# Pre-norm transformer layer, one core: more of the fourth batch's query projections in the first attention slot, LayerNorm passes earlier, output projections in three interleaved portions

## The chip, the cores and the metric

The kernel runs on one core of a Trainium2 chip. A core has a matrix engine (TensorE, PE in the profile, its weight loads PEld), a vector engine (VectorE, DVE), an activation engine (ScalarE, ACT), a general engine (GpSimd, POOL), a sequencer that issues most of the transfers here (SyncE, SP), and 16 DMA engines. Each engine runs its own instructions in the order in which they were written, and waits at an instruction until the semaphores that it names have the values it wants. SBUF is the on-chip memory; matmuls write to PSUM, a small memory of banks.

The metric is the time of one launch on the device in microseconds (us), the median of several runs; lower is better. The profile comes from one more execution, which has a time of its own.

## The reference

One transformer layer on x of 4 batches × 512 tokens × 512 channels, all in fp32:

```python
def reference(x, Wq, Wk, Wv, Wo, W_gate, W_up, W_down):
    x = x + attention(layernorm(x), Wq, Wk, Wv, Wo)
    x = x + ffn(layernorm(x), W_gate, W_up, W_down)
    return x

# attention: 32 query heads and 8 key/value heads of 16 channels, T = 512
q, k, v = (h @ Wq), (h @ Wk), (h @ Wv)          # 512x512, 512x128, 512x128
q, k = q * cos + rotate_half(q) * sin, k * cos + rotate_half(k) * sin
att = where(causal, q @ k.T / sqrt(16), -inf)   # four query heads share a key head
out = (softmax(att) @ v) @ Wo
# ffn: F = 1376
y = (silu(h @ W_gate.T) * (h @ W_up.T)) @ W_down.T
```

The layernorm has no scale or shift; eps is 1e-5.

## The kernel before

**The slots.** After an opening, attention runs in four *slots*, one for each batch (`slot(b, steps)`). A slot has eight *groups* of four heads, numbered 0 to 31 over all batches. A group has four *visits* and a `last_visit`, then `averages`. In a visit PE computes two kinds of scores into PSUM (`both_scores`): `plain` (L993), queries by keys, of the group two ahead, from which DVE only takes a minimum of each row (`greatest`, L1039; it becomes the softmax's shift), and `less` (L1006), keys by queries, of the current group, from which ACT takes the exponentials (`exponentials`, L1094) and POOL clears what is above the diagonal (`causal`, L1099). `averages` (L1121) multiplies the exponentials with the values; DVE later transposes the result and takes reciprocals (`read`, L1135 and L1138), and after each second group it turns the finished heads into `cx[m]` (four tiles `cx[0]` to `cx[3]`, one for two groups). `masked` (L978, POOL) prepares the queries of a group three ahead.

**The gaps.** After the scores of visit n stands `gap(n)`, in which PE does other work: a slot gets a list of *steps*, each with a cost in microseconds that was written by hand, and a gap takes steps from its front (`fill`) until the share `shares[n]` of the list's total is used up. In slot 0 there are four gaps to a group; in slots 1 to 3 there is a fifth, `gap(4)`, after the averages. Slot 0's list (`early`) holds projections of batches 1, 2 and 3 (`rest1`, `rest2`, `rest3`), slots 1 to 3 hold the output projection and the FFN of the batch whose attention is done. Slots 1 to 3 end their attention two groups ahead in the scores, so the list is what fills the rest of PE's time.

**A projection** (`projections`, `projected`): the normalised rows, transposed (`xnT`), by a weight, 512 × 128 at a time, in eight steps of 0.43 (four narrow matmuls, eight matmul records in the profile; L299). Keys come first, then the queries of the first part, the values, and the queries of parts 1 to 3. The finished product is rotated: DVE steps `sines` (L358) and `cosines`, with multiplications and additions on POOL (L359); the keys are then spread by four POOL operations (L425). These steps stand in the queue `full` until an odd moment takes them (`odd_steps`) or until a new product needs a bank (`emptied`).

**PSUM.** `bank()` (L187) gives a product one of three buffers (`ps_mm`, 512 columns each) for everything that is not scores or averages: projections, output projections, FFN. Six more such buffers' room goes to scores and averages.

**The LayerNorm of batch 2** is made in twelve passes on ACT with the power on POOL (`quietly`: sum a, square b, scale c for each of four tiles), which stand in `calm`; `odd_steps` takes one per call. That of batch 3 is made by DVE (`statistics`, L218; `normalised`, L226) with the power on POOL (L221); batches 1 and 3 are transposed by DVE and four writes to DRAM for each tile (`flipped`, L318, issued by SP), read back as `xnT` (L320). Batch 2 is transposed by PE (`turned2`).

**The output projection** (`attended`): for each of four token tiles i, four products m (`cx[m]` by `wo_sb`, 0.85 us each) into one bank, in two portions of 1.72; then DVE adds the result to the rows (`add`, L515), and statistics, normalisation and flip of that tile (`both_steps`) go to the queue `aside`. Each product first runs all that stands in `later` (the reading of the last averages and the turning into `cx`). For batch 0 the output projection stands in slot 1 (groups 8 on), for batch 1 in slot 2 (groups 16 on), for batch 2 in slot 3 (groups 24 on), for batch 3 in the last stage, which has no attention. The last queries of batch 3 (`rest3[-24:]`, parts 1 to 3) also stand at the front of slot 1, and before the FFN the first weights are loaded by SP (`load_f(0)`, L176).

Of the kernel before, what the change touches and what calls it, by code (L numbers as in the profile page):

```python
# [22 lines left out]
NT = T // P  # L23
# [51 lines left out]
def preln_block_kernel(  # L75
# [59 lines left out]
    first, second, one16, one0 = (rope_sb[:, 2 * T + n : 2 * T + n + 1] for n in range(4))  # L135
# [44 lines left out]
    thin = [True]  # L180
# [4 lines left out]
    def emptied(n):  # L185
        for _ in range(n):
            for _, step in full.popleft():  # L187
                step()

    def bank():  # L190
        emptied(max(len(full) - (2 if copied[0] else 1), 0))
        return ps_mm.tile([P, T], F32, tag="mm", name="mm")
# [6 lines left out]
    def load_xr(b, i):  # L199
        nc.sync.dma_start(out=xr[b, i], in_=x[b, ts(i, P), :])  # L200
# [13 lines left out]
    def statistics(src):  # L214
        st = small.tile([P, 6], F32, tag="st", name="st")
        mv = small.tile([P, 2], F32, tag="mv", name="mv")
        rstd = small.tile([P, 1], F32, tag="rstd", name="rstd")
        nc.vector.bn_stats(st, src)  # L218
        nc.vector.bn_aggr(mv, st)
        nc.vector.tensor_scalar(rstd, mv[:, 1:2], EPS, None, ALU.add)  # L220
        nc.gpsimd.tensor_tensor(rstd, rstd, neghalf, ALU.pow)  # L221
        return src, mv, rstd
# [24 lines left out]
    calm = deque()  # L247
# [3 lines left out]
    aside, later = deque(), deque()  # L251
# [3 lines left out]
    def do(queue, n=1):  # L255
        for _ in range(min(n, len(queue))):
            queue.popleft()[1]()
# [61 lines left out]
        for a in [i - 1, i] if i == last else [i - 1] if i > 0 else []:  # L319
            nc.sync.dma_start(out=dst[:, :, ts(a, P)], in_=flip[n].rearrange("(k p) t -> p k t", p=P)[:, :, ts(a, P)])  # L320

    def portions(products, finish, n=2):

        made = {}

        def part(a):
            if a == 0:
                made["ps"] = bank()
            for step in products[len(products) * a // n : len(products) * (a + 1) // n]:
                step(made["ps"])  # L330
            if a == n - 1:
                left = deque(finish(made["ps"]))
                if left:
                    full.append(left)
                if not thin[0]:
                    emptied(len(full))

        return [lambda a=a: part(a) for a in range(n)]
# [153 lines left out]
    def attended(b, by_pe=()):  # L492

        found, xn, ready = {}, {}, []

        def measure(i):
            found[i] = statistics(xr[b, i])

        def norm(i):
            xn[i] = work.tile([P, D], F32, tag="xa", name="xn", bufs=4)  # L500
            normalised(xn[i], found[i])

        def flip(i):
            if i not in by_pe:
                flipped(xn[i], i, b % 2, xnTs[0], last=NT - 1 - len(by_pe))
            ready.append(i)

        def outp(i):
            def product(ps, m):
                do(later, len(later))  # L510
                product_of(ps, cx[m][:, ts(i, P)], wo_sb[:, m, :], m == 0, m == 3)

            def finish(ps):
                def add():
                    nc.vector.tensor_tensor(xr[b, i], ps, xr[b, i], ALU.add)  # L515
                    aside.extend(both_steps(measure, norm, flip, [i]))

                return [(0.69, add)]

            return [(1.72, step) for step in portions([lambda ps, m=m: product(ps, m) for m in range(4)], finish)]  # L520

        def tail():
            while NT - 1 not in ready:
                do(aside)
            for i in by_pe:
                transposed(xn[i], i, xnTs[0])

        def begin():
            if b > 0:
                for i in range(NT):  # L530
                    load_xr(b, i)

        first = [(0.0, begin), *(step for i in range(NT) for step in outp(i))]
        return first, [(0.45 * len(by_pe), tail)]

    wgu = {}

    def load_f(f):
        if f < whole:
            wgu[f] = shared[:, (f + 2) % 3, :, :, :]  # L540
            for a, w in enumerate((wg, wu)):
                load_w(wgu[f][:, a, :, :], w[:, ts(f, P)])
# [76 lines left out]
    def after(step):  # L619
        return 0.0, step  # L620
# [552 lines left out]
    begin3, turned3, rest3, _ = projections(3, 3)  # L1173
    begin2, turned2, rest2, load2 = projections(2, 2)
    begin1, turned1, rest1, _ = projections(1, 1, then=load2)
    begin, turned, start, _ = projections(0, 0, early=True)
# [29 lines left out]
    def fill(steps, upto, done):  # L1206
        while steps and done + steps[0][0] / 2 <= upto:
            cost, step = steps.popleft()
            step()
            done += cost  # L1210
            if not thin[0]:
                do(aside)
        return done
# [5 lines left out]
    for h in range(2):  # L1219
        for n, entries in enumerate((((0, 3),), ((0, 2), (3 * P, 0)), ((0, 1),))):  # L1220
            for c, i in entries:
                for r in range(4):
                    plain_score(h, r, i, pairs[r // 2][:, r % 2, c : c + P * (i + 1)])
            for r in range(4):
                for c, i in entries:
                    greatest(h, r, i, pairs[r // 2][:, r % 2, c : c + P * (i + 1)])
            if n == 2:
                turned_round(h)
            odd_steps((1.5, 1.0, 2.7 - h)[n])
            if h == 0:  # L1230
                nc.gpsimd.memset(values(n + 1), 1.0)
            done = fill(opening, each * (h + (0.3, 0.68, 1.0)[n]), done)
        if h == 0:
            laid_out(0)
            masked(2)
# [3 lines left out]
    def slot(b, steps):  # L1239

        steps = deque(steps)
        total = sum(cost for cost, _ in steps)
        done, part = 0.0, 0.0
        groups = range(8 * b, 8 * b + 8)
        thin[0] = copied[0] = b == 0
        narrow[0] = True

        shares = (0.2, 0.225, 0.2875, 0.2875, 0.0) if thin[0] else (0.19, 0.19, 0.22, 0.22, 0.18)

        def upcoming(n):  # L1250

            upto, us = part + total * shares[n] / 8, 0.0
            for cost, _ in steps:
                if done + us + cost / 2 > upto:
                    break
                us += cost
            return us

        def gap(n):
            nonlocal done, part  # L1260
            part += total * shares[n] / 8
            pool_steps((3, 2, 2, 0, 3)[n])
            done = fill(steps, part, done)

        for g in groups:
            h = g + 2
            laid_out(g + 1)
            for n, visit in enumerate(visits):
                e = (e0, e0, e1, e1)[n]
                if h < len(GROUPS):  # L1270
                    both_scores(h, g, visit)
                    exponentials(e[:, slice(0, 2) if n % 2 else slice(2, 4), :], less)
                elif n % 2 == 0:
                    both_scores(h, g, visit)
                    exponentials(e[:, 2:4, :], less)
                    exponentials(e[:, 0:2, :], plain)
                if n == 1:
                    causal(e0, 0)
                if n == 3:
                    causal(e1, 0)  # L1280
                    causal(e1, 3 * P, exchanged=True)
                all_greatest(h, visit)
                holding[0] = n == 3
                if thin[0]:
                    odd_steps((1.3, 0.95, 0.95, 1.05)[n], (2, 1, 1, 0)[n])
                else:
                    odd_steps(min(0.8 * upcoming(n) - (0.4, 0.4, 0.8, 0.8)[n], 2.3))
                gap(n)
            last_visit(h, g)
            turned_round(h)  # L1290
            averages(g)
            odd_steps(1.4)
            if not thin[0]:
                gap(4)
        thin[0] = copied[0] = narrow[0] = False
        emptied(len(full))
        if b == B - 1:
            do(later, len(later))
        for cost, step in steps:
            step()  # L1300
# [9 lines left out]
    def restored():  # L1310
        nc.scalar.dma_start(out=homes[1], in_=spill)

    turns = [step for pair in zip(turned2, *[iter(rest1[-8:])] * 2) for step in pair]
    early = [*rest1[16:-8], *turns, begin3, *rest2, *turned3, *rest3[:-24]]
    for u in range(whole):
        early.insert(4 * u + 4, after(lambda u=u: copies(u)))
    slot(0, early)
# [1 line left out]
    before, behind = attended(0, by_pe=(2, 3))  # L1319
# [18 lines left out]
    for u in range(whole):  # L1338
# [3 lines left out]
        asides += [(at + 1.0 * n, lambda n=n, combine=combine: combine(n)) for n in range(4)]  # L1342
    asides += [(6.0, spilled), (34.0, load_down), (34.1, load_rest)]
    start1 = [
        before[0],
        *rest3[-24:-12],
        *before[1:],
        after(lambda: load_f(0)),
        *rest3[-12:-1],
        *behind,  # L1350
        rest3[-1],
# [16 lines left out]
    before, behind = attended(1)  # L1368
# [15 lines left out]
    before, behind = attended(2)  # L1384
# [3 lines left out]
    before, behind = attended(3)  # L1388
# [36 lines left out]
```

## Time and profile before

| what | value |
|---|---|
| time, median of 3 runs (lowest to highest) | 847.44 us (846.82 to 847.46) |
| time of the profiled execution | 848.06 us |
| span of the profiled execution | 845.8 us |
| granted TensorE clock, mean | 1.00 |
| opening, until group 0's first scores | 0 to 49.8 us |
| slot 0 (groups 0 to 7) | 49.8 to 173.6, 123.8 us |
| slot 1 (groups 8 to 15) | 173.6 to 357.7, 184.1 us |
| slot 2 (groups 16 to 23) | 357.7 to 536.0, 178.3 us |
| slot 3 (groups 24 to 31) | 536.0 to 667.5, 131.5 us |
| last stage | 667.5 to 845.8, 178.3 us |

A line of the timeline has the start in us, the duration in us, the engine, the line of the code, the operation, its output and input by the program's names with their shapes, and how many instructions are drawn together; in brackets the engine's idle time just before it and what ended it. "SPq" is the queue of SyncE. PE instructions that follow each other at once on several parts of the array are drawn with overlapping times.

### The profile page before, as it was taken

What the parts mean: (1) busy time and instruction counts of PE and PEld (TensorE: products, weight loads), DVE (VectorE), ACT (ScalarE), POOL (GpSimd) and SP (SyncE); (2) the same over time, 40 slices, a digit from 0 to 9 for tenths busy, and PEclk for the clock granted to TensorE, in tenths of its full rate; (3) what the DMA queues carried; (4) which work ended last, traced back from release to release, by engine and by line L of the source; (5) the groups of instructions that cost most, each with busy time, mean ns of one, the idle gap of its engine ahead of it and who ended that gap; (6) DMA issues with size and microseconds to landing.
All of it is one profiled execution on the core that took longest, in us unless ns stands there. A gap on an engine that the chain in (4) does not pass through costs nothing.

```text
span 845.8 us, 28256 instructions
## 1 busy us (share of the span) xinstructions
PE 822.5 (97%) x11980; PEld 452.2 (53%) x11980; DVE 545.5 (65%) x1601; ACT 231.3 (27%) x342; POOL 352.5 (42%) x514
## 2 busy tenths in 40 slices
PE   6999999999999999999999999999999999999998
PEld 5654444544333335333555555436655556788887
DVE  7877777778555554458677776686877633656632
ACT  1045654422232322222233232222323331011100
POOL 4575574773544344223265634532244444101130
PEclk9999999999999999999999999999999999999999
DMA  8533304003764742253344632325333534545811
GB/s 259 124 96 78 91 16 91 5 3 64 232 191 144 235 137 77 88 200 77 84 155 140 196 115 66 115 47 151 96 97 103 162 106 148 119 146 174 291 33 50
DMA packets 149517, 101.57 MB, mean 120 GB/s; under 512 B 59696, under 2 KB 137264, under 8 KB 149136
## 3 DMA queue, kind: packets, MB, share of 16 engines
q1 hardware_dynamic: 149104, 94.01, 38.3%
q10 hardware_dynamic: 288, 5.77, 1.8%
q8 instruction: 94, 1.54, 0.8%
q14 instruction: 31, 0.25, 0.1%
HBM read 78.32 MB, written 25.17 MB: 122 GB/s over the span
## 4 chain that ended last, share of the span: by engine, by line
PE 76%; DVE 12%; POOL 4%; DMA 3%; issue 2%; ACT 1%; SPq 1%; POOLq 0%; DVEq 0%; ACTq 0%
PE mm L299 38%; PE mm L296 14%; PE sc L993 12%; DVE junk L1039 6%; PE av L1121 6%; PE sc L1006 4%; PE mm L590 2%; POOL e L1099 1%; DMA shared<-packed 1%; PE mm L582 1%; DVE st L218 1%; DVE rot L358 1%; ACT e L1094 1%; POOL home L425 1%; POOL qa L978 1%
## 5 line engine op out<-in xcount | busy, mean ns | idle before, releaser
L1039 DVE CUSTOM_DVE_ANT_0 junk<-sc,mask 128x128 f32<-128x128 f32 (+3 forms) x512 | 251.2, 491 | 139.0 <-PE sc L1006 78.4
L1094 ACT ACTIVATE e<-sc 128x1024 f32<-128x1024 f32 (+1 forms) x192 | 165.5, 882 | 384.4 <-PE sc L1006 300.7
L299 PE MATMUL mm<-xnT,shared 128*32 128x256 f32 (+1 forms) x3520 | 244.2, 420 | 2.3 <-DMA shared<-in_wg 1.5
L1099 POOL TENSOR_SCALAR_AFFINE_SELECT e<-e 128x512 f32<-128x512 f32 (+2 forms) x192 | 105.7, 560 | 225.4 <-ACT e L1094 222.3
L299 PEld LDWEIGHTS mm<-xnT,shared 128*32 128x32 f32 x3520 | 116.9, 110 | 113.0 <-issue 62.8
L993 PE MATMUL sc<-home,qa 32*64 32x512 f32 (+6 forms) x2048 | 156.1, 421 | 6.5 <-DVE low L1039 3.0
L1006 PE MATMUL sc<-qa,home 32*64 32x512 f32 (+6 forms) x2048 | 152.2, 427 | 1.5 <-DVE low L1039 0.8
L993 PEld LDWEIGHTS sc<-home,qa 32*64 32x64 f32 x2048 | 66.8, 131 | 90.2 <-DVE low L1039 29.1
L1121 PE MATMUL av<-e,home 128*32 128x512 f32 (+3 forms) x1024 | 81.9, 438 | 1.8 <-POOL e L1099 1.6
L296 PE MATMUL mm<-xnT,shared 128*128 128x256 f32 x360 | 80.3, 383 | 1.0 <-DMA shared<-packed 1.0
L296 PEld LDWEIGHTS mm<-xnT,shared 128*128 128x128 f32 x360 | 68.3, 192 | 12.8 <-issue 2.2
L299 PE MATMUL mm<-wd_sb,home 128*32 128x256 f32 (+3 forms) x848 | 71.4, 470 | 0.0
L1006 PEld LDWEIGHTS sc<-qa,home 32*64 32x64 f32 x2048 | 58.8, 130 | 22.5 <-issue 8.7
L1121 PEld LDWEIGHTS av<-e,home 128*32 128x32 f32 x1024 | 30.5, 109 | 47.2 <-issue 35.0
L299 PEld LDWEIGHTS mm<-wd_sb,home 128*32 128x32 f32 (+1 forms) x848 | 28.2, 110 | 36.9 <-issue 28.2
L299 PE MATMUL mm<-wo_sb,cx 128*32 128x512 f32 x384 | 45.4, 595 | 0.0
L797 POOL TENSOR_TENSOR wd_sb<-home 128x256 f32<-128x256 f32 x15 | 11.4, 759 | 75.6 <-DVE home L721 75.3
L1039 DVE DVE_READ_ACCUMULATOR2_ANT low<- 128x1 f32 x512 | 42.4, 83 | 0.0
L221 POOL TENSOR_TENSOR rstd<-rstd,neghalf 128x1 f32<-128x1 f32 x24 | 16.0, 667 | 56.8 <-DVE rstd L220 56.7
L1145 POOL TENSOR_TENSOR inv<-us,inverse 128x256 f32<-128x256 f32 x32 | 20.9, 654 | 44.5 <-DVE inverse L1138 44.3
L359 POOL TENSOR_TENSOR rot<-rot,rope_sb 128x512 f32<-128x512 f32 x18 | 25.7, 1425 | 23.0 <-DVE rot L358 22.8
L721 POOL TENSOR_TENSOR home<-home,u 128x512 f32<-128x512 f32 x20 | 25.2, 1281 | 21.2 <-DVE u L757 21.2
(146 smaller groups left out, 855.6 us busy)
## 6 DMA issues: line engine op xcount, KB each, us to landing
shared<-packed SPq DMA_DIRECT2D x90, 256.0 KB
flip<-u SPq DMA_DIRECT2D x88, 64.0 KB
packed<-xnT SPq DMA_DIRECT2D x10, 512.0 KB
xnT<-flip SPq DMA_DIRECT2D x18, 256.0 KB
wd_sb<-differences SPq DMA_DIRECT2D x7, 640.0 KB
shared<-packed SPq DMA_DIRECT2D x30, 128.0 KB
rows<-in_x SPq DMA_DIRECT2D x14, 256.0 KB
out<-rows SPq DMA_DIRECT2D x13, 256.0 KB
```

The costliest lines, as they stand in the source:

```text
L296: nc.tensor.matmul(out, lhsT=lhsT, rhs=rhs, start=start, stop=stop)
L299: nc.tensor.matmul(out[c : c + 32], lhsT=lhsT[:, c : c + 32], rhs=rhs, start=start, stop=stop)
L359: put(lambda: engine.tensor_tensor(rot, rot, sin, ALU.mult))
L590: nc.tensor.matmul(ps[96:P, ts(q, P)], lhsT=rest_w[:, a, kq, 32 * q : 32 * q + 32], rhs=xnTs[0][:, kq, most:], start=kq == 0, stop=kq == N ...
L721: engine.tensor_tensor(g, g, t, ALU.mult)
L993: nc.tensor.matmul(dst[at : at + 64, :n], lhsT=qa[g][rows_of(r), q : q + 64], rhs=keys_of(g)[rows_of(r), :n], start=True, stop=True,)
L1006: nc.tensor.matmul(dst[at : at + 64, first_q:], lhsT=keys_of(g)[rows_of(r), k : k + 64], rhs=qa[g][rows_of(r), P * j + first_q :], start=True,
L1039: nc.vector.tensor_tensor_reduce(out=junk[:, :n], in0=src, in1=mask[:, T - n : T] if i else mask[:, T:], scale=-1.0, scalar=BIG, op0=ALU.a ...
L1094: nc.scalar.activation(dst, src, AF.Exp, scale=1.0 / math.sqrt(DH))
L1099: nc.gpsimd.affine_select(out=e[rows, heads, c : c + P], in_=e[rows, heads, c : c + P], compare_op=ALU.is_ge, fill=0.0, base=base, pattern ...
L1121: nc.tensor.matmul(av[32 * r : 32 * r + 32, P * j :], lhsT=v[:, j, 4 * (m // 2) + r, DH * (1 - hf) : DH * (3 - hf)], rhs=e[:, r, c : c + n ...
L1145: nc.gpsimd.tensor_tensor(us[m][:, :, hf, :], turned[0][:, :, hf, :], by, ALU.mult)
```

## The change

There are five edits.

1. `rest3[-24:-12]`, the queries of part 1 and the first four steps of part 2 of batch 3, move from the front of slot 1 to the end of slot 0's list.
2. Slot 0 gets the fifth gap, `gap(4)` after the averages, with a share of 0.07; the other shares go down accordingly.
3. The twelve LayerNorm passes of batch 2 are taken from `calm` in the opening, up to four for each of its score visits, ahead of slot 0. Batch 1's list is split in another place: PE's transposes of batch 2 (`turned2`) are woven into its steps 28 to 35 instead of its last eight, and `begin3` (the loads and LayerNorm of batch 3) follows them.
4. An output projection is made in three portions, of two, one and one products; the portions of the four tiles are interleaved, so that a tile's last product (m = 3, the last heads) stands behind the next tile's first three. Only the product m = 3 still runs all that stands in `later`.
5. In slot 1 `load_f(0)` goes first.

```diff
-    def portions(products, finish, n=2):
+    def portions(products, finish, n=2, cuts=None):
         made = {}
         def part(a):
             if a == 0:
                 made["ps"] = bank()
-            for step in products[len(products) * a // n : len(products) * (a + 1) // n]:
+            lo, hi = ((0, *cuts, len(products))[a + k] if cuts else len(products) * (a + k) // n for k in (0, 1))
+            for step in products[lo:hi]:
                 step(made["ps"])
...
         def outp(i):
             def product(ps, m):
-                do(later, len(later))
+                if m == 3:
+                    do(later, len(later))
                 product_of(ps, cx[m][:, ts(i, P)], wo_sb[:, m, :], m == 0, m == 3)
...
-            return [(1.72, step) for step in portions([lambda ps, m=m: product(ps, m) for m in range(4)], finish)]
+            parts = portions([lambda ps, m=m: product(ps, m) for m in range(4)], finish, 3, (2, 3))
+            return list(zip((1.72, 0.86, 0.86), parts))
...
-        first = [(0.0, begin), *(step for i in range(NT) for step in outp(i))]
+        parts = [outp(i) for i in range(NT)]
+        first = [(0.0, begin), *parts[0][:2]]
+        for i in range(1, NT):
+            first += [*parts[i][:2], parts[i - 1][2]]
+        first.append(parts[-1][2])
         return first, [(0.45 * len(by_pe), tail)]
...
             done = fill(opening, each * (h + (0.3, 0.68, 1.0)[n]), done)
+            for _ in range(min(4, len(calm))):
+                calm.popleft()()
...
-        shares = (0.2, 0.225, 0.2875, 0.2875, 0.0) if thin[0] else (0.19, 0.19, 0.22, 0.22, 0.18)
+        shares = (0.19, 0.21, 0.265, 0.265, 0.07) if thin[0] else (0.19, 0.19, 0.22, 0.22, 0.18)
...
             odd_steps(1.4)
-            if not thin[0]:
-                gap(4)
+            gap(4)
...
-    turns = [step for pair in zip(turned2, *[iter(rest1[-8:])] * 2) for step in pair]
-    early = [*rest1[16:-8], *turns, begin3, *rest2, *turned3, *rest3[:-24]]
+    turns = [step for pair in zip(turned2, *[iter(rest1[28:36])] * 2) for step in pair]
+    early = [*rest1[16:28], *turns, begin3, *rest1[36:], *rest2, *turned3, *rest3[:-12]]
...
     start1 = [
-        before[0],
-        *rest3[-24:-12],
-        *before[1:],
         after(lambda: load_f(0)),
+        *before,
         *rest3[-12:-1],
```

`after(step)` makes a step of no cost; `before` is the output projection's list, whose first entry loads rows of x (`begin`), and `behind` its closing transposes.

## The prediction

> **What bounds the kernel now.** I read the page's shares and chain first, then the stages by windows, then single gaps in the timeline.
>
> ```profile
> span 845.8 us, 28256 instructions
> ...
> PE 822.5 (97%) x11980; PEld 452.2 (53%) x11980; DVE 545.5 (65%) x1601; ACT 231.3 (27%) x342; POOL 352.5 (42%) x514
> ...
> PE 76%; DVE 12%; POOL 4%; DMA 3%; issue 2%; ACT 1%; SPq 1%; POOLq 0%; DVEq 0%; ACTq 0%
> ```
>
> PE is busy 97% of the span, so moving work pays only where PE waits. DVE's 12% of the chain is what it waits for most. The windows (length, then busy time of PE, PEld, DVE, ACT, POOL, then clock, DMA share, GB/s) show where, for slots 0 and 1:
>
> ```profile
> 49.80:173.60 123.80, 116.62 (x2322) 57.96 (x2321) 90.88 (x319) 66.06 (x107) 80.46 (x117) 1.00 0.25 62
> 173.60:357.70 184.10, 182.18 (x2524) 70.57 (x2525) 106.97 (x349) 48.43 (x60) 82.27 (x121) 1.00 0.45 134
> ```
>
> Slot 0 has 7.2 us without PE, slot 1 only 1.9. A visit of slot 0:
>
> ```profile
> 97.51 1.50 PE L299 MATMUL mm<-xnT,shared 128*32 128x256 f32 x24
> 97.62 0.69 DVE L1039 CUSTOM_DVE_ANT_0 junk<-sc,mask 128x512 f32<-128x512 f32 x1 [0.17 <-PE sc L1006]
> ...
> 98.36 0.69 DVE L1039 CUSTOM_DVE_ANT_0 junk<-sc,mask 128x512 f32<-128x512 f32 x1
> ...
> 98.97 0.08 DVE L1039 DVE_READ_ACCUMULATOR2_ANT low<- 128x1 f32 x1
> ...
> 99.11 0.65 PE L993 MATMUL sc<-home,qa 32*64 32x512 f32 x2
> ```
>
> The three steps between two score visits (24 records) start at 97.51, the next scores at 99.11, just after DVE's minima end at 99.05: this gap is set by DVE. At 159.83 only two steps stand in such a gap, and it lasts 1.60 us all the same. In slot 1 it is otherwise:
>
> ```profile
> 205.97 3.66 PE L299 MATMUL mm<-xnT,shared 128*32 128x256 f32 x64
> ...
> 208.71 0.51 SPq L176 DMA_DIRECT2D shared<-in_wg  x1
> ...
> 209.56 0.54 PE L993 MATMUL sc<-home,qa 32*64 32x384 f32 x2
> ...
> 213.63 1.92 PE L299 MATMUL mm<-xnT,shared 128*32 128x512 f32 x16 [1.46 <-DMA shared<-in_wg]
> ```
>
> Eight steps (64 records) take 3.6 us, and the next scores (209.56) follow at once: work added here is added to the span. The lines at 208.71 and 213.63 show a late weight load: issued at 208.71 behind four flips and two xnT reads on SP, it holds PE 1.46 us.
>
> **The change, part by part.** A step is eight matmul records; 64 records in 3.6 us against 32 in about 1.8 (gaps of slot 1) give 0.43 us a step.
>
> (1) Twelve steps leave slot 1: 12 × 0.43 = -5.15.
>
> (2) The load of the first gate and up weights now stands first in slot 1, ahead of the flips. The gap of the 1.46 us wait lasted 4.97 us (210.51 to 215.48) for 2.99 of work and 0.17 of turnaround: -1.8. If the load came late again it would be 0, the upper bound. Its two issues (0.51 us each) pass on SP when only rows of x are asked for, which nothing needs for 15 us. The second load was and is issued over 4 us ahead of need.
>
> (3) Slot 0. The twelve steps go four into visits (groups that had 13 or 14 steps get the 3, 3, 4, 4 that others had) and eight into the new gap after the averages. For the visits the cover is DVE's four minima; steps of 1.28 and 1.71 stand in gaps of 1.60 and 2.06. At the group's end the averages take 2.55 instead of the 2.18 of slot 1, and the next scores 1.36 instead of 1.05 (waits for POOL's masked queries and for DVE): 3.91 us, where averages, a step with its turnaround and scores need 2.18 + 0.63 + 1.05 = 3.86. So I price the twelve at 0; without that cover at 12 × 0.43 = +5.15, the upper bound. Other steps move within slot 0. The keys' POOL burst at 121.44 delays the causal mask to 124.41, and that group's averages took 4.02 instead of 2.57; one visit earlier and one group later it finds slack: -1.45. The first group's averages, 0.95 over the others behind POOL's late rotations, lose that wait too: -0.95; small rests -0.2.
>
> Against this stand two delays. All 12 LayerNorm passes of batch 2 now stand on ACT (with POOL's powers) ahead of the first exponentials. The rows:
>
> ```profile
> 42.58 0.63 ACT L234 ACTIVATE rows<-xa 128x512 f32<-128x512 f32 x1 [19.35 <-DMA xa<-in_x]
> ...
> 51.06 1.02 ACT L1094 ACTIVATE e<-sc 128x1024 f32<-128x1024 f32 x1 [6.68 <-PE sc L1006]
> ```
>
> From 42.58 four first passes of 0.86 with their scaling, four second of 0.78 and four third of 0.75 make 9.6 us, and the third tile's waits for POOL's power (1.34 us queued behind rotations of 1.27 that begin at 47.12) add one to two. The first exponential moves from 51.06 to about 53.8, and PE's second visit, which needs the pair of score banks it reads, from 52.5 to about 55.1: +2.7 (0 to 3). And batch 3's flip to DRAM falls about four steps before the keys that use it rather than about 13 us before: the writes take 2 us to issue (117.63, 1.97) and land about 3.9 us after their start; the two reads land 2.0 to 4.5 later. Data about 12.5 us after the group's start, the key step that needs both about 11: +1.4 (0 to +3.9). Part 3: -1.45 - 0.95 - 0.2 + 2.7 + 1.4 = +1.5.
>
> (4) The border to slot 1. Three rotary steps (0.69 to 0.74 each) are now flushed together with the averages' read (0.72 + 0.25) in front of the first minima of group 8; before, two. The averages end 6.6 us into the group, DVE is through at 7.5: +0.95 (0 to 1.3).
>
> (5) Output projections in three portions, interleaved. PE's work is unchanged: four products of 0.85 for each of four tiles. But a product needs one of three PSUM buffers of its kind, and in group 8 one is kept by batch 3's half-finished queries, one by tile 0, one by tile 1, now open together. Tile 2 opens only when tile 0's residual add (L515, 0.65) has read its buffer, and tile 3 when tile 1's has. Each add stands on DVE behind the visit's four minima (1.9 us, ending about 1.9 after the scores), so it ends about 2.7 after them; the 0.85 of work before it ends at 0.95. PE waits 1.85 twice: +3.7 (3.0 to 4.0). Queued behind on PE are the rest of the projections and the next scores, and for these ACT. Before, tile followed tile and the free buffer hid the add.
>
> (6) The adds come in pairs now, and each brings statistics (0.70, 0.18, 0.15), a normalisation (0.54) and a flip (0.70) on DVE. In group 9 two visits get 5 to 6 us of these before their last minima, while PE brings 3 to 4: two stalls, 0.6 and 0.9 by the sums of durations: +1.5 (0 to 2.3).
>
> (7) Slot 2 has the same: at group 16 tile 2 waits for tile 0's add (+0.85, the queue being shorter), in group 17 the queue of normalisation, flip, add, statistics, a final sum (0.69) and normalisation is 4.1 us ahead of the minima (+2.2); the stalls of before there (0.45 and 0.27) go: +2.35 (0.8 to 3). Such a wait of before shows at 395.67:
>
> ```profile
> 395.67 0.69 PE L1006 MATMUL sc<-qa,home 32*64 32x256 f32 x16 [0.21 <-DVE low L1039]
> ```
>
> (8) Slot 3: tile 2 finds a free buffer, no bank wait, but group 25's queue holds two adds and their trains, 5.1 us: a stall of 1.5 where before had 0.14: +1.35 (0 to 1.7).
>
> (9) The last projections after slot 3: PE waits for no head there now (0.0 us idle from 667.5 to 700), so nothing is gained: 0.
>
> Sum: -5.15 - 1.8 + 1.5 + 0.95 + 3.7 + 1.5 + 2.35 + 1.35 = +4.4. The profiled execution took 848.06 (span 845.8 and 2.26 around it): 852.46; it lies 0.62 above the median 847.44, so 851.8.
>
> [...] The windows show a granted clock of 1.00 throughout, also from 205 to 216 with the 1.46 us wait. [...]
>
> **The rivals.** A, the other side: DVE's queue does not reach PE. The 9.85 of terms 4 to 8 vanish: 851.8 - 9.85 = 842.0; from 4.4 of it on, the change is not slower. For it: DVE is busy 58% of slot 1 (106.97 of 184.10), and a stall lets it catch up, so my stalls may not add. Against: the order on DVE is fixed, and the add stands behind the minima wherever the buffer is needed. B: slot 0 doesn't hide the twelve steps: 857.0. For it: PE is busy 94% of that slot, and 0.05 us of margin covers the eight border steps; against: the gap at 159.83 that didn't shrink with fewer steps. C: batch 3's turn through DRAM lands at its upper bound: +2.5, 854.3. For it: 4.5 us reads stand in the trace; against: the queue is nearly empty there (DMA share 0.11 from 108.8 to 128).
>
> **How the numbers follow.** Forecast 0.60, A 0.17 (any loss of half the queue's price or more), B 0.11, C 0.12. The forecast's own range, its bounds not all at one end, is 848.7 to 855. A reaches below and B above; to leave out two in ten I take 847.3 to 855.9. This kernel can't be told from no change within 0.2%, 1.7 us: 845.7 to 849.1. Faster needs most of A: 0.11. Same takes the rest of A and the forecast's low end: 0.15. Slower: 0.74.
>
> **What would show it.** In the profile after: the slot 0 window 1 to 2 us longer, with a first exponential near 53.8; no wait for the gate weights in slot 1; PE waits of about 1.85 us for "rows L515" before two output projections in group 8, one near group 16; waits for "low L1039" in groups 9, 17 and 25. If slot 1 shrinks by about 7 and slots 2 and 3 stay, A holds and the forecast is wrong. If slot 0 grows by 5 and more, B or C.

## The result and the profile after

The changed kernel takes 855.99 us (median of 6 runs, 855.32 to 860.33) against 847.45 us for the kernel before (6 runs, 846.82 to 848.69): ratio 1.0112, 95% interval 1.0086 to 1.0138. It is slower by about 8.5 us; the forecast was 4.4, and the time lies 0.1 us above the forecast's range. The profiled execution took 855.35 us with a span of 853.5, against 848.06 and 845.8. From the page after, the engines and the chain of waits:

```profile
PE 823.8 (97%) x11980; PEld 453.1 (53%) x11980; DVE 546.1 (64%) x1601; ACT 232.4 (27%) x343; POOL 353.1 (41%) x514
...
PE 80%; DVE 13%; DMA 3%; issue 2%; ACT 1%; POOL 0%; SPq 0%; DVEq 0%; POOLq 0%; ACTq 0%
```

The work is the same to the last matmul; what grew is waiting, and, as will be seen, matmuls at half clock, which count as busy. The windows of the profile after, cut at the first scores of group 0 and where the averages of groups 7, 15 and 23 end (columns as in the prediction; the clock stands third from the end):

```profile
50.70:178.20 127.50, 120.19 (x2411) 61.58 (x2414) 91.61 (x321) 62.62 (x95) 84.42 (x118) 0.99 0.25 60
178.20:358.70 180.50, 174.35 (x2412) 66.61 (x2408) 104.85 (x341) 48.56 (x60) 77.49 (x116) 1.00 0.46 137
358.70:541.30 182.60, 178.41 (x3054) 88.06 (x3050) 125.57 (x371) 50.40 (x69) 75.01 (x109) 0.99 0.40 124
541.30:853.50 312.20, 307.61 (x3826) 205.39 (x3817) 182.87 (x445) 61.37 (x96) 88.78 (x131) 1.00 0.41 122
```

Cut at the same places, the profile before has its borders at 49.8, 173.6, 354.9 and 533.2. Against the forecast's terms:

| stage | before | after | measured | forecast |
|---|---|---|---|---|
| opening | 49.8 | 50.7 | +0.9 | 0 |
| slot 0 | 123.8 | 127.5 | +3.7 | +1.5 (part 3) |
| slot 1 | 181.3 | 180.5 | -0.8 | -0.8 (parts 1, 2, 4, 5, 6) |
| slot 2 | 178.3 | 182.6 | +4.3 | +2.35 (part 7) |
| slot 3 and last stage | 312.6 | 312.2 | -0.4 | +1.35 (parts 8, 9) |

The table ahead of the prediction cuts at the scores that follow, behind the work of the fifth gap (178.8, 361.5 and 544.1 in the profile after). With those borders slot 0 grew by 4.3 and slot 1 shrank by 1.4; the other rows stay the same.

**Slot 1.** The group of the output projection's matmuls on the page before and on the page after (the last number is PE's idle time ahead of them), and the waits in the timeline after (the number in brackets is PE's idle time and what ended it):

```profile
L299 PE MATMUL mm<-wo_sb,cx 128*32 128x512 f32 x384 | 45.4, 595 | 0.0
...
L299 PE MATMUL mm<-wo_sb,cx 128*32 128x512 f32 x384 | 45.5, 596 | 4.0 <-DVE rows L517 4.0
```

```profile
184.09 0.65 PE L1000 MATMUL sc<-home,qa 32*64 32x512 f32 x2 [1.47 <-DVE low L1046]
...
190.72 0.69 DVE L517 TENSOR_TENSOR rows<-mm,rows 128x512 f32<-128x512 f32 x1
...
191.46 2.78 PE L299 MATMUL mm<-wo_sb,cx 128*32 128x512 f32 x24 [1.60 <-DVE rows L517]
...
197.03 0.69 DVE L517 TENSOR_TENSOR rows<-mm,rows 128x512 f32<-128x512 f32 x1
...
197.77 1.92 PE L299 MATMUL mm<-wo_sb,cx 128*32 128x512 f32 x16 [1.60 <-DVE rows L517]
...
383.07 1.49 PE L299 MATMUL mm<-wo_sb,cx 128*32 128x512 f32 x12 [0.79 <-DVE rows L517]
```

Tile 2 and tile 3 each start 0.05 us after the residual add that frees their buffer, as read from the code (it has three buffers for products; scores and averages take five more, L171 and L173, not six). The first line is the border wait behind DVE's rotations, the last the wait for a buffer behind group 16.

**Slot 0.** The first exponentials, and what PE does while they are late:

```profile
54.86 0.81 ACT L402 ACTIVATE xa<-xa,mean,rstd 128x512 f32<-128x512 f32 x1 [0.51 <-POOL mean L244]
...
55.58 1.00 ACT L1101 ACTIVATE e<-sc 128x1024 f32<-128x1024 f32 x1
...
56.63 0.65 PE L1013 MATMUL sc<-qa,home 32*64 32x512 f32 x2 [2.17 <-ACT e L1101]
```

The last LayerNorm pass stands directly ahead of the first exponential; the visit took 4.28 us instead of 1.05. Later, in group 5, batch 3's transposed rows are late:

```profile
142.58 0.64 PE L299 MATMUL mm<-xnT,shared 128*32 128x256 f32 x8 [1.83 <-DMA xnT<-flip]
...
144.17 3.92 PE L1128 MATMUL av<-e,home 128*32 128x512 f32 x32
```

The second line is the surprise. These averages take 2.18 us in the neighbouring groups, and they wait for nothing here. The windows around them (busy PE is the first number behind the length):

```profile
140.70:142.60 1.90, 0.07 (x8) 0.06 (x5) 0.60 (x5) 0.00 (x0) 1.82 (x3) 1.00 0.44 130
142.60:144.00 1.40, 1.40 (x40) 0.79 (x40) 0.00 (x0) 0.00 (x0) 1.32 (x3) 0.98 0.04 12
144.00:147.00 3.00, 3.00 (x24) 0.79 (x20) 1.77 (x9) 1.09 (x2) 1.49 (x3) 0.50 0.00 0
```

PE is idle to 142.6, and from 144.0 the granted clock is 0.50 until 147.4: PE counts as busy for all of the 3.00 us, and the averages take 3.92 instead of 2.18. By half-microsecond windows the stretch loses 1.71 us of clock. A second one lies from 403.4 to 406.8, behind a wait of 2.53 us for "low L1046" in group 17 (its windows stand below, under "When the clock falls").

The kernel before has neither. The twelve steps, on the other hand, are hidden. Groups 1, 2, 3 and 6 of slot 0 last 15.1 to 15.3 us in both kernels, with a step more at the border (averages 2.18, step 0.6, scores 1.17, where there were 2.55 and 1.36).

### The profile page after: what moved, and what is told of

It is laid out like the page before. It is cut to its first block, busy times and chain, and to the rows that moved or that the text cites. A ratio compares the mean times of both kernels' runs of the same rounds, so it can differ in the third digit from the quotient of the medians.

```text
span 853.5 us, 28260 instructions
## 1 busy us (share of the span) xinstructions
PE 823.8 (97%) x11980; PEld 453.1 (53%) x11980; DVE 546.1 (64%) x1601; ACT 232.4 (27%) x343; POOL 353.1 (41%) x514
## 4 chain that ended last, share of the span: by engine, by line
PE 80%; DVE 13%; DMA 3%; issue 2%; ACT 1%; POOL 0%; SPq 0%; DVEq 0%; POOLq 0%; ACTq 0%
PE mm L299 36%; PE mm L296 17%; PE sc L1000 12%; PE av L1128 8%; DVE junk L1046 8%; PE sc L1013 4%; PE mm L597 2%; PE mm L589 1%; DMA flip<-u 1%; DVE rot L359 1%; DVE st L218 1%; PE mm L304 1%; DVE u L314 0%; DVE rows L517 0%; DVE home L363 0%
## 5 line engine op out<-in xcount | busy, mean ns | idle before, releaser
L1046 DVE CUSTOM_DVE_ANT_0 junk<-sc,mask 128x128 f32<-128x128 f32 (+3 forms) x512 | 251.2, 491 | 154.6 <-PE sc L1013 90.4
L1046 DVE DVE_READ_ACCUMULATOR2_ANT low<- 128x1 f32 x512 | 42.4, 83 | 0.0
```

The costliest lines, as they stand in the source:

```text
L1046: nc.vector.tensor_tensor_reduce(out=junk[:, :n], in0=src, in1=mask[:, T - n : T] if i else mask[:, T:], scale=-1.0, scalar=BIG, op0=ALU.a ...
```

## The experiments

### Where the interleave costs: undo it, restrict it, do it alone

Undone, with all the rest of the change kept:

```diff
-                if m == 3:
-                    do(later, len(later))
+                do(later, len(later))
...
-            parts = portions([lambda ps, m=m: product(ps, m) for m in range(4)], finish, 3, (2, 3))
-            return list(zip((1.72, 0.86, 0.86), parts))
+            return [(1.72, step) for step in portions([lambda ps, m=m: product(ps, m) for m in range(4)], finish)]
...
+        first = [(0.0, begin), *(step for i in range(NT) for step in outp(i))]
```

> The changed kernel with only the output projections put back (two portions, tile after tile, every product flushing the waiting averages). Theory (the interleaved projections stall PE on PSUM buffers and bunch DVE's work): the waits of 1.96 us twice in group 8 are replaced by one wait of 1 to 2 us for the last heads, group 9's 1.41 and 0.60 fall to about 0.5, group 17's 1.21 and 2.75 go back to about 0.6 and 0.4, the half-clock stretch behind it (1.74) goes, group 25's 1.29 goes: about 10 us less, 844 to 847. Rival (DVE lags there anyway, because the twelve steps left slot 1 and the adds come earlier): within 2 us of the changed kernel, 854 to 856.

Measured 847.46 us against 847.66 (0.9994, 0.9981 to 1.0007): some 8.5 us less than the changed kernel. Slot 1 lasts 176.9 (180.5), slot 2 178.2 (182.6). The waits for buffers are gone, one for the last heads stands instead:

```profile
185.68 1.07 PE L299 MATMUL mm<-wo_sb,cx 128*32 128x512 f32 x8 [2.07 <-DVE cx L1152]
```

So the rest of the change is about neutral as a whole, and the interleave is what makes it slower. It left the late first exponentials and the late rows with their half clock in slot 0 (the rows' wait is even longer in this execution, 3.16 us against 1.83).

For batch 0 alone (`if b > 0:` takes the old order):

> The changed kernel with the interleaved output projections for batch 0 alone (slot 1); batches 1 to 3 as before. Theory (pairs of adds bunch DVE's work in groups 17 and 25 also where a buffer is free): group 17's 1.21 and 2.75 go back to about 0.6 and 0.4, the half-clock stretch behind it (1.7) goes, group 25's 1.29 goes: 5 to 6 less, about 850. Rival (all of the cost is the full buffers in slot 1): 855 to 856.

852.58 us against 847.84 (1.0050, 1.0035 to 1.0064). Group 17's waits went back to those of before, group 25's went, and slot 2 lasts 178.2: there the interleave cost 4.4, as the theory said. The total fell by 3.4 by the medians rather than 5 to 6. Slot 3 gave nothing (172.5 and 172.6 us for groups 24 to 31), so group 25's wait had only taken the place of smaller ones, and in the profiled execution group 5 is 0.95 longer, its wait for the rows being 2.84.

As the only edit on the kernel before:

> The kernel before with the interleaved output projections as its only edit; the twelve steps stay at the front of slot 1. Theory (two parts to the cost of the interleave: full buffers, which depend on what else holds one, and pairs of adds on DVE in slots 2 and 3, which don't): in slot 1 about 0.9 for tile 2's buffer in group 8's last gap, since a product of another tile now covers half of the wait, and little for tile 3; in slot 2 group 17's 1.21 and 2.75 in place of 0.6 and 0.4, and mostly a half-clock stretch of 1.7; in slot 3 group 25's 1.3: 5 to 8 more than before, 853 to 856. Rival (the interleave hurts only together with the moved steps): within 2 us of before, and no wait over 1 us in groups 17 and 25.

853.24 us against 848.21 (1.0065, 1.0047 to 1.0082). Slot 1 grows by 3.8 and slot 2 by 2.7. Two waits of its trace:

```profile
190.31 1.92 PE L299 MATMUL mm<-wo_sb,cx 128*32 128x512 f32 x16 [0.81 <-DVE rows L517]
...
215.57 2.28 PE L299 MATMUL mm<-xnT,shared 128*32 128x512 f32 x12 [2.25 <-DVE wd_sb L363]
```

The buffer's wait is 0.81, near the 0.9 expected; the wait of 2.25 in group 9, with a half-clock stretch behind it, was not. Group 17 had its wait again (2.54, in the changed kernel 2.53), this time with no half clock. The interleave hurts by itself: 5.0 alone, 8.5 on top of the other edits.

### Full buffers and late rows: eight steps instead of twelve

```diff
-    early = [*rest1[16:28], *turns, begin3, *rest1[36:], *rest2, *turned3, *rest3[:-12]]
+    early = [*rest1[16:28], *turns, begin3, *rest1[36:], *rest2, *turned3, *rest3[:-16]]
...
-        *rest3[-12:-1],
+        *rest3[-16:-1],
```

> The changed kernel with eight steps moved instead of twelve, so that no half-finished product holds a PSUM buffer across the border of the slots, and batch 3's keys come some 3 us later. Theory (buffers, and data of batch 3 late): group 8's two waits of 1.96 go (-3.9), group 5's 1.83 for the transposed rows and the half-clock stretch of 1.6 behind it go (-3.4), four steps come back to slot 1 (+1.7): about 5.6 less, 850 to 851. Rival (DVE's queue makes the waits of group 8, whatever buffer is free): 1.7 less at most by group 5, and waits of 1.5 and more stay in group 8: 854 and more.

851.63 us against 847.66 (1.0041, 1.0028 to 1.0055), 4.4 less than the changed kernel. No wait for a buffer is left in group 8, though the adds still stand behind minima on DVE there: with a buffer free, that order alone doesn't hold PE. The rows of batch 3 are in time, and no half clock follows; slot 0 falls from 127.5 to 124.3. The border's wait (1.46 for DVE) stays.

### The LayerNorm passes

Ten of them in the opening:

```diff
-            for _ in range(min(4, len(calm))):
+            for _ in range(min(4, max(len(calm) - 2, 0))):
```

> The changed kernel with the last two LayerNorm passes of batch 2 left out of the opening's visits (ten passes there instead of twelve); they are taken by the first odd moments of slot 0. Theory (the first exponentials stand behind all twelve passes on ACT): first exponential near 52 instead of 55.58, group 0's wait of 3.24 us falls below 1, total 2 to 3 us less, about 853. Rival (the two passes only move behind the first exponential and delay the next one): no more than 0.5 us less, 855 to 856.

855.55 us against 847.66 (1.0079, 1.0048 to 1.0111): slot 0 as long as in the changed kernel (group 0 is 0.7 us shorter, group 5, with a wait of 2.52 for the rows, 0.65 longer). The first exponential does come at 52.50 instead of 55.58, but PE then waits in the next visits:

```profile
55.20 1.29 POOL L360 TENSOR_TENSOR rot<-rot,rope_sb 128x512 f32<-128x512 f32 x1
```

```profile
57.89 0.01 DVE L423 LOAD_MASK_SELECT ks<-kr  x1 [1.33 <-POOL kr L364]
...
60.41 0.54 PE L1000 MATMUL sc<-home,qa 32*64 32x384 f32 x2 [0.91 <-DVE low L1046]
```

The passes' powers stand on POOL ahead of the keys' rotation (55.20, in the kernel before 50.44); DVE waits for the keys with the next minima behind that wait, and PE for the minima. ACT was one of two queues that were held up; the theory had named one. With six passes left out (in `best8_ln6`, below) both are free, but the opening and slot 0 together end only 0.2 us earlier there. With none in the opening (`max(len(calm) - 12, 0)`, on the last version below):

> As the last, but with no LayerNorm pass of batch 2 taken in the opening's visits. Theory (some passes must be early, or the transposes of batch 2 wait for them): waits of 2 us and more in groups 0 and 1, 845 and more. Rival (the odd moments suffice): no wait in group 0 beyond those of the kernel before, 841 to 843.

851.87 us (1.0050, 1.0031 to 1.0070). PE's transposes of batch 2 wait for the passes, and two half-clock stretches follow (from 69.6 and from 76.4):

```profile
69.64 1.12 PE L304 MATMUL mm<-ident,xa 128*128 128x128 f32 x4 [2.06 <-ACT xa L402]
...
76.52 1.11 PE L304 MATMUL mm<-ident,xa 128*128 128x128 f32 x4 [2.55 <-ACT xa L402]
```

So some passes must be early. Twelve hold back the first exponentials, but no run shows a gain in the total from taking fewer.

### The early weight load by itself

```diff
     start1 = [
-        before[0],
-        *rest3[-24:-12],
-        *before[1:],
         after(lambda: load_f(0)),
+        before[0],
+        *rest3[-24:-12],
+        *before[1:],
```

> The kernel before with one edit only: the load of the first gate and up weights stands first in slot 1. Theory (SP's queue delayed that load): the wait of 1.46 us near 213 goes and nothing else changes, 1.8 less, 845.6. Rival (the load is late for another reason, or the flips behind it are late instead): within 0.5 us of before.

847.47 us against 847.66 (1.0001, 0.9991 to 1.0011): the rival. The load is issued at 181.19 and nobody waits for it, and PE stands all the same:

```profile
213.37 0.69 DVE L307 COPY xnT<-mm 128x512 f32<-128x512 f32 x1
...
214.16 1.92 PE L299 MATMUL mm<-xnT,shared 128*32 128x512 f32 x16 [1.05 <-DVE xnT L307]
```

The copy of the last transposed tile stands behind four minima on DVE and ends at 214.06. The same product needs it; the late load had covered it.

### When the clock falls

Added DVE work in groups 10 to 15 of the kernel before:

```diff
+                if 10 <= g < 16 and n % 2:
+                    for _ in range(g - 7 if n == 3 else 18 - g):
+                        extra = work.tile([P, T], F32, tag="junk", name="junk")
+                        nc.vector.tensor_tensor(extra, mask[:, :T], mask[:, :T], ALU.add)
                 all_greatest(h, visit)
```

> The kernel before with three to eight added DVE instructions of about 0.7 us ahead of the minima of the second and of the fourth visit of groups 10 to 15 (rising with the group in the fourth visit, falling in the second), so that PE waits from near 0 to about 4 us at twelve places. Nothing it computes changes. Theory from the changed kernel's trace (half-clock stretches of 3.4 us behind waits of 1.83 and 2.75, none behind 1.2 to 1.96 in group 8): a stretch behind most of the waits over about 2.5 us, behind some from 1.8 to 2.5, behind none below 1.4, each costing 1.6 to 1.8 us. Rival (the clock falls at any time, whatever PE waits for): as many stretches behind short waits as behind long ones. [...]

878.73 us (one run). Four half-clock stretches, 1.71 us of clock lost in each, behind waits of 5.3, 3.6, 3.2 and 3.9 us; none behind 2.5, 2.4, 2.2, 2.1 and 1.6. Two waits in the windows, the first with the 3.4 us of work behind it:

```profile
258.00:261.60 3.60, 0.15 (x6) 0.01 (x3) 3.39 (x7) 0.60 (x1) 3.37 (x5) 1.00 0.56 155
261.60:265.00 3.40, 3.40 (x44) 1.42 (x48) 2.05 (x8) 1.02 (x1) 0.55 (x1) 0.52 0.55 179
286.80:290.20 3.40, 1.23 (x12) 0.13 (x4) 3.19 (x7) 0.17 (x1) 3.05 (x4) 1.00 1.04 396
```

Behind the long one 1.71 us of clock are lost on top; behind the short one the clock stays 1.00. The clock does follow the waits, though not from the length that the theory expected. Taken over the 14 profiled executions of this study (PE's idle time from the end of one matmul, by its size, to the start of the next; 49 to 800 us): of 28 waits of 1 to 2 us none has a stretch behind it, of 19 waits of 2 to 3 us eight have, of 7 over 3 us all have. The kernel before has no wait over 1.65, the changed kernel three from 2.0 to 2.7.

The length alone doesn't decide. Group 17's wait, in the changed kernel (the 3.41 us ahead of the fall and the 3.41 behind it) and then in `outp_alone` (half-microsecond windows from its start on):

```profile
399.95:403.36 3.41, 1.01 (x36) 0.72 (x40) 2.87 (x10) 0.00 (x0) 1.73 (x3) 1.00 0.61 171
403.36:406.77 3.41, 3.41 (x30) 1.26 (x32) 1.94 (x9) 1.08 (x2) 1.49 (x3) 0.50 0.33 52
```

```profile
399.50:400.00 0.50, 0.11 (x4) 0.00 (x0) 0.50 (x1) 0.00 (x0) 0.50 (x1) 1.00 0.79 123
400.00:400.50 0.50, 0.00 (x0) 0.00 (x0) 0.50 (x2) 0.00 (x0) 0.50 (x2) 1.00 0.37 66
400.50:401.00 0.50, 0.00 (x0) 0.00 (x0) 0.47 (x3) 0.00 (x0) 0.43 (x2) 1.00 0.48 115
401.00:401.50 0.50, 0.00 (x0) 0.00 (x0) 0.47 (x3) 0.00 (x0) 0.50 (x1) 1.00 1.02 310
401.50:402.00 0.50, 0.00 (x0) 0.00 (x0) 0.47 (x3) 0.00 (x0) 0.04 (x1) 1.00 1.12 406
402.00:402.50 0.50, 0.35 (x16) 0.35 (x24) 0.50 (x3) 0.00 (x0) 0.00 (x0) 1.00 0.51 193
402.50:403.00 0.50, 0.50 (x32) 0.31 (x16) 0.22 (x1) 0.00 (x0) 0.00 (x0) 1.00 0.00 0
403.00:403.50 0.50, 0.50 (x12) 0.16 (x8) 0.00 (x0) 0.21 (x1) 0.00 (x0) 1.00 0.00 0
```

The first wait, 2.53 us, is followed by 3.41 us at 0.50 and loses 1.71 more; the second, 2.54 us, loses nothing: the clock stays 1.00. What sets the two apart no run here shows. For a wait of 2 to 3 us the length alone therefore doesn't tell whether 1.71 us come on top.

### A version that is faster than both

Old projections, eight steps moved, the next eight ahead of the projections (`*rest3[-16:-8]` at the front of slot 1):

> The kernel with the output projections as before, eight steps moved instead of twelve, and the other eight steps of a whole product at the front of slot 1, ahead of the output projection; the rest of the change stays. Theory (the moved steps are hidden, and what the undone projections still leave is batch 3's late rows with its half clock, 4.7 us in groups 5 and 6, and the wait for the last heads, 2.4 in group 8): from 847.5 about 4.7 and 2.4 less and 1.7 more for the four steps, 842. Rival (the waits come back in another place, since DVE is full in groups 8 and 9): 845 and more.

850.03 us against 847.84 (1.0031, 1.0017 to 1.0045): a miss. Slot 0 shrank as expected (123.4), but a wait of 3.33 appeared in group 9, with a half-clock stretch of twice the usual length behind it (3.4 us of clock lost). The same with six passes in the opening (`len(calm) - 6`):

> The same, with only six of the twelve LayerNorm passes in the opening and six at the odd moments of slot 0, as before. Theory (the passes on ACT and their powers on POOL hold the first exponentials and the rotations): group 0's wait of 3.2 us falls below 1, so 2 to 3 less than its neighbour, 839 to 840. Rival (the transposes of batch 2, which stand early in the list, then wait for the late passes): no less than its neighbour, and waits on ACT in groups 0 and 1.

846.88 us (0.9993, 0.9978 to 1.0009): 3.1 less than its neighbour, by the medians. The first exponentials are in time (51.44 instead of 53.78), but the passes are not what the profiled executions differ by: slot 0 ends at 173.0 instead of 173.2, and group 9 is 3.5 shorter, mostly because no half clock follows its wait this time. The level stays high because of that wait:

```profile
211.02 1.92 PE L299 MATMUL mm<-xnT,shared 128*32 128x512 f32 x16 [2.74 <-DMA xnT<-flip]
```

Eight steps ahead of the projections push them back, and leave four fewer behind them, before the FFN needs the flipped rows. Hence seven steps moved, five ahead, twelve behind:

```diff
-    early = [..., *rest3[:-16]]
+    early = [..., *rest3[:-17]]
...
-        *rest3[-16:-8],
+        *rest3[-17:-12],
         *before[1:],
-        *rest3[-8:-1],
+        *rest3[-12:-1],
```

> Output projections as before, six LayerNorm passes in the opening, and seven steps moved instead of eight: the last step of that product and the next four stand at the front of slot 1. Theory (at the border DVE is late because the finished product's rotation is flushed into it there; in group 9 PE waits 3.4 us because too few steps stand between the last residual add and the transposes of its rows): group 8's 1.69 goes, group 9's 3.41 falls to the 1.6 of the kernel before, one step (0.43) comes back to slot 1: 843 to 844.5. Rival (DVE has the same work in groups 8 and 9 and only meets PE elsewhere): 846 and more.

844.95 us against 847.75 (0.9960, 0.9945 to 0.9975): faster than both kernels, by 0.4% against the one before, and 0.45 above the range expected. Its windows for slots 0 and 1, with nothing at a lower clock:

```profile
50.30:174.00 123.70, 116.91 (x2371) 60.37 (x2374) 92.11 (x321) 62.58 (x96) 84.52 (x118) 1.00 0.26 62
174.00:352.70 178.70, 177.04 (x2454) 67.83 (x2448) 104.41 (x341) 48.59 (x60) 77.32 (x116) 1.00 0.46 138
```

Group 8 has no wait at the border: the product is finished after the first minima of slot 1, and so is its rotation. With the copy of the transposed tile on ACT (`if i % 2 and not thin[0] and not narrow[0]` in `transposed`):

> The same, and in slots 1 to 3 the copy of the last transposed tile out of PSUM is made by ACT instead of DVE. Theory (group 9's remaining wait, 1.6 us, which the early load of the gate weights alone didn't remove, is this copy standing behind four minima on DVE): about 1 us less than its neighbour, 842 to 843.5, and no wait over 0.8 in group 9. Rival (the wait is for the residual add and statistics before the transposes): no change against its neighbour.

844.57 us (0.9957, 0.9941 to 0.9974), the same as its neighbour within the intervals: the wait in group 9 had already fallen to 0.26 there, and is 0.16 here. The rival's figure holds; its reason, the residual add and the statistics, was not tested.

## Why the prediction was wrong in its size

**The step that failed** is the price of a wait: each one entered the sum at its own length. What stood behind that was a clock of 1.00 around one wait of 1.46 us; the forecast put waits of up to 2.7 us into the kernel and priced them the same way. The trace shows half-clock stretches that lose 1.71 us each behind two of these, the late rows of group 5 and DVE's queue in group 17: 3.4 us together. The profiled execution is 7.3 over the one before, the forecast's sum was 4.4. The half clock's 3.4 and the opening's 0.9, which the last section puts down to the start of the execution, were not in the sum; its other terms came out 1.4 lower together. Not every such wait had a stretch behind it: around the wait of 2.17 us in group 0 the clock stays 1.00 (53.0 to 60.5).

Point by point:

- **Part 1, twelve steps, -5.15, hidden in slot 0:** held. Groups without another wait kept their 15.2 us.
- **Part 2, the weight load, -1.8:** the reason was incomplete. Alone the load gave nothing that can be measured; a DVE copy is due at the same place. In the changed kernel that copy ends at 215.51 and the product starts at 220.84 with no wait, so the wait is gone, but not by the load alone.
- **Part 3, +1.5:** measured +3.7, or +4.3 with the borders of the prediction. The gain on the delayed mask came as sized (group 4 lasts 15.2 instead of 16.6). The first exponentials: +2.7 expected, the visit took 3.2 more, and POOL's queue is part of it. The late rows: +1.4 expected, 1.83 measured by the profile (2.0 from the modelled end of the last matmul). The half clock behind them, 1.7, was not in the sum.
- **Parts 4 to 6, slot 1:** border 0.95 expected, 1.47 measured; buffers 1.85 twice expected, 1.60 by the trace's count and 1.8 from start to start less the 0.85 of work; group 9 1.5 expected, 0.62 and 0.20 by the trace's count. That the stage came out at -0.8 is in part luck: border and group 9 err in opposite directions, and by the prediction's borders it is -1.4.
- **Part 7, slot 2:** the waits were right (0.79 at group 16 for 0.85; 2.53 in group 17 for 2.2); the half clock behind the second wait makes the stage 4.3 instead of 2.35.
- **Part 8, slot 3, +1.35:** the wait came (1.05 for "low L1046" at 578.86), but groups 24 to 31 grew by 0.1 only: group 24 is 1.8 shorter, group 25 1.8 longer.
- **Rivals:** A (DVE's queue not reaching PE) and B (steps not hidden) are refuted by `undo_outp` and by the groups of slot 0; C's mechanism was real, at a size between forecast and bound.

What stays open: the six runs spread from 855.3 to 860.3 with mean clocks of 0.991 to 0.998. The profiled execution's 0.996 is its two stretches; that the others have one to some four of them is an inference from the mean, and which waits they stand behind no trace shows.

## What to carry to other kernels

Opening a second accumulation before the first is drained saves a wait only while a buffer is free: in the changed kernel PE waited 1.60 us twice in group 8, and in `whole8`, with one buffer more free there, for none. Count who holds each buffer at that place, half-finished products of other work included, and place the drain's engine queue beside it. A wait of 2 us and more on the matrix engine is not priced by its length: look for the clock in the windows behind it. Here 8 of 19 waits of 2 to 3 us and 7 of 7 above 3 had a stretch behind them, which lost 1.71 us more, in `best8` 3.4. Work that is moved early is queued on every engine it uses; the second queue (here POOL) can hold what the first no longer does: in `ln_ten` the first exponential came at 52.50 instead of 55.58, and then DVE waited 1.33 us for POOL's keys and PE 0.91 us for the minima behind them.

## What was not expected of the hardware

The clock fell behind waits of 2.0 us and up, in 8 of 19 cases between 2 and 3 us and in 7 of 7 above, and each stretch of 3.41 us lost 1.71 us. The length of the wait did not sort the cases between 2 and 3 us: behind 2.53 us in group 17 of the changed kernel the clock fell, behind 2.54 us in the same group of `outp_alone` it did not. And the opening, 0.9 us longer, has the same program up to there: its first matmuls of 256 columns start 0.43 us apart, later ones 0.215. In the profile before that changes at 12.4 us after three of them, in the profile after at 14.3 after eight:

```profile
11.02 8.67 PE L296 MATMUL mm<-xnT,shared 128*128 128x256 f32 x32
```

The kernel before needs 7.66 us for the same line. The clock's record begins at the same places, 12.35 and 14.24 us, with full clock; ahead of them it has no entry, for which the windows print 1.00, so this half rate is seen in the starts alone. The opening lasted 49.8 us in the kernel before, 50.3 in `best7_ln6` and 50.7 in the changed kernel; those 0.9 us are more than some of the edits are worth.
